# Layer 0 and feed-forward: short-row matmuls replaced by full 128-row f32r matmuls over stacked halves

## The chip, the cores and the metric

The kernel runs on one core of a Trainium2 chip. The metric is the time of one execution on the device, in microseconds. The engines that matter here, by the names of the profile: PE (TensorE, matmuls), ACT (ScalarE), DVE (VectorE), POOL (GpSimd) and SP, whose queue issues most of the transfers. Each engine works through its own queue in order.

## The reference

Four images of 128 channels and 64 x 64 pixels go through two layers. Cut to what matters (layer 1 is attention with a feed-forward, and then a recurrence along the tokens):

```python
# layer 0, on the group-normalised image
e1  = prelu(w1 @ x + b1, a1)          # 64 x 4096
e2  = prelu(w2 @ x + b2, a2)          # 64 x 4096
asm = prelu(wa @ x + ba, aa)          # 128 x 4096
score = softmax(einsum('nci,ncj->nij', e1, e2), axis=2)
x = x + einsum('nij,ncj->nci', score, asm)
# layer 1, on tokens (4096 per image): 16 heads of 8, then
x1 = ln(x + attn_out, g1, beta1)
zf = cos(x1[..., :8]) * cos(ry_theta)
h  = relu(zf @ w1.T + b1)             # 8 -> 512
out = ln(x1 + h @ w2.T + b2, g2, beta2)
```

The scores of layer 0 contract over 64 channels, and the first matmul of the feed-forward contracts over 8.

## The kernel before

The images are taken one after the other, and each has two stages.

**Layer 0** (`first_stage`, which calls `layer0`). The image lies as 128 channels x 4096 tokens. It is normalised (L340), and then two 1x1 convolutions give e1 and e2, in four pairs of 512-column blocks each (L352; the pairs' PSUM tiles are called pca and pcb). Each uses the 64 weights twice over, so that both halves of the 128 partitions hold the same 64 rows. `prelu` is two relus on ACT (L303, L304) and one combining step on DVE (L305). A third convolution gives asmT, with tokens on partitions: a bias matmul of one row (L360) and then the product (L369). `prelu_vector` (L309, L310) does every other one of its prelus on DVE alone.

Then come eight blocks `ic` of 512 tokens. For each, 16 steps `jp` compute the scores of 2 x 128 other tokens (L396, into a pair of PSUM banks called s), take their exponential on ACT (L404, tile p), add p up on DVE (L409, L412), and multiply p by asmT (`weigh`, L419, into acc). Two steps' scores stand together, followed by the two earlier steps' weighing. The scores are f32 matmuls of 64 rows; j = 0 uses partitions 0 to 63 and j = 1 uses 64 to 127.

Into this loop other work is woven by calls of `meanwhile`, which the code counts: the own block's normalisation and transposes (`tokens`), and, for images 1 to 3, the feed-forward of the image before (`feed_forward`, stepped by `step_late`, from the call after the twelfth on). The feed-forward's first matmul is L1049, its second L1060:

```python
            for j in range(2):
                rows = ds(32 * (f0 + j), D)
                nc.tensor.matmul(phs[j], f1_sb[rows, :], zT[rows, :], start=True, stop=True)
```

D is 8: eight rows of weights against 512 tokens, in eight chunks per image. Its ACT relu is L1052, the tile is hT.

**Attention** (`second_stage`, `attention`): scores of four heads in 32-row tiles of f32r (L879), exponentials on ACT (L891), transposes on DVE (L698), and two kinds of weighted sums on PE (L711, L732). At the end of the stage, POOL adds up the parts of each of three blocks of queries (`mirrored`: L774 copies, L759, L799 copies and L801 additions, in tiles called other, room and own). This runs on beside the start of the next image's layer 0, and the results are taken up there at three counted calls of `meanwhile`.

After the last image come its own feed-forward (`third_stage`), `fold_norm`, and the recurrence.

The engines' order in layer 0 is the order of the program (`tc.manual_schedule`). Every stage lays its tiles in SBUF anew, so a tile lies where earlier stages had others, and its first writer waits for the last user of those bytes. The first tiles of the layer-0 stage are the feed-forward's, then a tile called gap that nothing uses:

```python
        rest = dict(e=(BIG, 2), big=(BIG, 1), mid=(MID, 5))
        pools = {**ffn, "gap": ((P, GAP), 1), **rest, **sums}
```

Of the kernel before, what the change touches and what calls it, by code (L numbers as in the profile page):

```python
# [26 lines left out]
def kernel(  # L27
# [103 lines left out]
    GAP = 12 * IC  # L131
# [14 lines left out]
    def load_twice(ap, name, axis):  # L146

        shape = list(ap.shape)
        shape[axis] *= 2
        t = const.tile(shape, F32, tag=name, name=name)  # L150
        for i in range(2):
            part = t[:, ts(i, CR)] if axis else t[ts(i, CR), :]
            nc.gpsimd.dma_start(out=part, in_=ap)
        return t


    w1_sb, w2_sb = load_twice(w1T, "w1_sb", 1), load_twice(w2T, "w2_sb", 1)
    b1_sb, b2_sb = load_twice(b1, "b1_sb", 0), load_twice(b2, "b2_sb", 0)
    wa_sb = load(waT, "wa_sb")
    a1_sb, a2_sb, aa_sb = load_row(a1, "a1_sb"), load_row(a2, "a2_sb"), load_row(aa, "aa_sb")  # L160

    ba_row = const.tile([33, P], F32, tag="ba_row", name="ba_row")
    for i in range(2):
        nc.gpsimd.dma_start(out=ba_row[ds(32 * i, 1), :], in_=ba)
    for t in (a1_sb, a2_sb, aa_sb):
        nc.vector.tensor_scalar(t, t, -1.0, None, ALU.mult)
    minus_b = []
    for i, b in enumerate((b1_sb, b2_sb)):
        t = const.tile([P, 1], F32, tag=f"minus_b{i}", name=f"minus_b{i}")
        nc.vector.tensor_scalar(t, b, -1.0, None, ALU.mult)  # L170
        minus_b.append(t)
# [18 lines left out]
    f1_sb = const.tile([P, P], F32, tag="f1_sb", name="f1_sb")  # L190
    ry_sb = once.tile([P, 1], F32, tag="ry_sb", name="ry_sb")
    nc.gpsimd.memset(f1_sb, 0.0)
    nc.gpsimd.memset(ry_sb, 0.0)
    for f in range(NF):
        nc.scalar.dma_start(out=f1_sb[ds(32 * f, D), :], in_=f1T[:, ts(f, P)])
        nc.scalar.dma_start(out=ry_sb[ds(32 * f, D), :], in_=ry)
    fb1_sb, f2_sb, fb2_bc = load(fb1, "fb1_sb"), load(f2T, "f2_sb"), load_row(fb2, "fb2_bc")
    g1_bc, be1_bc = load_row(g1, "g1_bc"), load_row(be1, "be1_bc")
    g2_bc, be2_bc = load_row(g2, "g2_bc"), load_row(be2, "be2_bc")
    W_sb, WT_sb, VT_sb = load(W, "W_sb"), load(WT, "WT_sb"), load(VT, "VT_sb")  # L200
# [3 lines left out]
    nc.vector.tensor_tensor(fb2_bc, fb2_bc, be1_bc, ALU.add)  # L204
    ident = const.tile([P, P], F32, tag="ident", name="ident")
# [91 lines left out]
    nc.vector.tensor_scalar(f1_sb, f1_sb, cry, None, ALU.mult)  # L297
# [35 lines left out]
    def layer0(n, xs, xh, norm, shifted, begin, meanwhile):  # L333
# [11 lines left out]
        for e, w, b, a, name in (  # L345
            (e1, w1_sb, (b1_sb, minus_b[0]), a1_sb, "a"),
            (e2, w2_sb, (b2_sb, minus_b[1]), a2_sb, "b"),
        ):
            for i in range(NIC // 2):
                pc = pair_psum(f"pc{name}{n}_{i}")  # L350
                for j in range(2):
                    nc.tensor.matmul(pc[:, j, :], w, xh[:, ts(2 * i + j, IC)], start=True, stop=True)  # L352
                y, z = mid_tile(f"y{name}{n}_{i}"), mid_tile(f"z{name}{n}_{i}")
                prelu(e[:, ts(i, 2 * IC)].rearrange("p (a b) -> p a b", a=2), pc, y, z, b, a)
                meanwhile()
        asmT = big_tile(f"asmT{n}")
        for i in range(NIC // 2):
            pc = pair_psum(f"pa{n}_{i}")
            for j in range(2):
                nc.tensor.matmul(  # L360
                    pc[:, j, :],
                    ones[ds(32 * j, 1), :],
                    ba_row[ds(32 * j, 1), :].unsqueeze(1).broadcast_to([1, TG, P]),
                    start=True,
                    stop=False,
                    skip_group_check=True,
                )
            for k in range(2 * TG):
                nc.tensor.matmul(  # L369
                    pc[:, k // TG, ts(k % TG, P)],  # L370
                    xh[:, ts(2 * TG * i + k, P)],
                    wa_sb,
                    start=False,
                    stop=True,
                    skip_group_check=True,
                )
            to = asmT[:, ts(i, 2 * IC)].rearrange("p (a b) -> p a b", a=2)
            if i % 2:
                prelu_vector(to, pc, mid_tile(f"za{n}_{i}"), aa_sb)
            else:  # L380
                prelu(to, pc, mid_tile(f"ya{n}_{i}"), mid_tile(f"za{n}_{i}"), (0.0, 0.0), aa_sb)
            meanwhile()

        if shifted:

            nc.vector.memset(e2[CR : CR + 1, :], 1.0)
            for ic in range(NIC):
                row_max(n, ic, e1, e2)
        state = {}

        def scores(ic, jp):

            s = pair_psum(f"s{n}_{ic}_{jp}")
            for j in range(2):
                rows = slice(0, CR + 1) if shifted else ts(j, CR)
                nc.tensor.matmul(  # L396
                    s[:, j, :],
                    e2[rows, ts(2 * jp + j, P)],
                    e1[rows, ts(ic, IC)],
                    start=True,  # L400
                    stop=True,
                )
            p = mid_tile(f"p{n}_{ic}_{jp}")
            nc.scalar.activation(p, s, AF.Exp)  # L404
            if jp == 0:
                state["first"] = p
            elif jp == 1:
                total = get("sums", f"total{n}_{ic}")
                nc.vector.tensor_tensor(total, state["first"], p, ALU.add)  # L409
                state[ic] = total  # L410
            else:
                nc.vector.tensor_tensor(state[ic], state[ic], p, ALU.add)  # L412
            return p
# [20 lines left out]
        before = []  # L434
        for ic in range(NIC):
            for jp in range(0, NP, 2):
                fresh = [(ic, j, scores(ic, j)) for j in (jp, jp + 1)]
                for i in range(2):
                    if before:
                        weigh(*before[i])  # L440
                        if before[i][1] == NP - 1:
                            take(before[i][0])
                            begin(before[i][0], state)

                    meanwhile(2 if ic == NIC - 1 else 1)
                before = fresh
# [5 lines left out]
    def row_max(n, ic, e1, e2):  # L452

        maxima = once.tile([P, TG, 4], F32, tag="mx", name=f"mx{n}_{ic}")
        for it in range(TG):
            for jb in range(4):
                s = pair_psum(f"sm{n}_{ic}_{it}_{jb}")
                for j in range(2):
                    nc.tensor.matmul(
                        s[:, j, :],  # L460
                        e1[:CR, ts(TG * ic + it, P)],
                        e2[:CR, ts(2 * jb + j, IC)],
                        start=True,
                        stop=True,
                    )
                nc.vector.tensor_reduce(maxima[:, it, jb : jb + 1], s, AX.XY, ALU.max)
        nm = once.tile([P, TG], F32, tag="nm", name=f"nm{n}_{ic}")
        nc.vector.tensor_reduce(nm, maxima, AX.X, ALU.max, negate=True)
        pm = one_psum(f"pm{n}_{ic}")
        for k in range(TG):  # L470
            nc.tensor.matmul(
                pm[CR : CR + 1, ts(k, P)], nm[:, k : k + 1], ident, start=True, stop=True
            )
        nc.vector.tensor_copy(e1[CR : CR + 1, ts(ic, IC)], pm[CR : CR + 1, :])
# [509 lines left out]
    def feed_forward(im, i, t2_rows, last, final):  # L984
# [37 lines left out]
        be1_z = be1_bc[:, 0:D].unsqueeze(1).broadcast_to([P, TG, D])  # L1022
        nc.vector.tensor_tensor(z, blocks(v)[:, :, 0:D], be1_z, ALU.add)
        steps = cos_steps(zr, z, zk, zr)
        for _ in range(3):
# [6 lines left out]
        nc.vector.tensor_copy(  # L1032
            zs.rearrange("p (k r d) -> p k r d", k=TG, d=D),
            zr.unsqueeze(2).broadcast_to([P, TG, P // D, D]),
        )
# [4 lines left out]
        nc.scalar.copy(zT, pz)  # L1040
# [3 lines left out]
        for f0 in range(0, NF, 2):  # L1044
            phs = [one_psum(f"ph{n}_{i}_{f}") for f in range(f0, f0 + 2)]
            hs.append(get("hT", f"hT{n}_{i}_{f0}"))
            for j in range(2):
                rows = ds(32 * (f0 + j), D)
                nc.tensor.matmul(phs[j], f1_sb[rows, :], zT[rows, :], start=True, stop=True)  # L1049
# [57 lines left out]
    def fold_norm():  # L1107
# [88 lines left out]
    def first_stage(im, before):  # L1196
# [7 lines left out]
        rest = dict(e=(BIG, 2), big=(BIG, 1), mid=(MID, 5))  # L1204
# [3 lines left out]
        with stage(f"conv{n}", **pools, **psum), tc.manual_schedule(engines=engines):  # L1208
# [4 lines left out]
            def meanwhile(steps=1):  # L1213

                calls[0] += 1
                if before and calls[0] in (13, 16, 19):
                    before["left"].pop(0)()
# [3 lines left out]
                for _ in range(0 if calls[0] <= 12 else 2 if calls[0] % 8 == 0 else 1):  # L1221
                    step_late()
# [21 lines left out]
    def second_stage(im, tail, upcoming):  # L1244
# [5 lines left out]
            denom=((P, 2 * NT + NQB // 2 * TG, 2), 2),  # L1250
            later=((P, NT * 32), 2),
# [3 lines left out]
            fixed=((P,), 1),  # L1255
# [50 lines left out]
    def hold_every():  # L1306

        pool = ends.enter_context(tc.tile_pool(name="every", bufs=1))
        held["every"] = pool.tile([P, N, S], F32, tag="every", name="every")
        for n in range(N - 1):  # L1310
# [30 lines left out]
    with stage("fold", half=(HALF, 1), ps_one=(ONE, 1)):  # L1341
        fold_norm()
# [103 lines left out]
    with tc.If(any_bad > 0):  # L1446
# [5 lines left out]
        with stage(  # L1452
# [7 lines left out]
            fold_norm()  # L1460
# [90 lines left out]
```

## Time and profile before

| | |
|---|---|
| three runs | 7282.81, 7290.19 and 7290.84 us, median 7290.19 |
| span of the profiled execution, first to last instruction | 7288.0 us |
| PE busy | 7006.0 us, 96% of the span |
| DVE, ACT, POOL busy | 5902.5, 6018.3 and 2838.9 us |
| mean granted clock of PE | 0.982 |
| layer 0 of image 0 | about 20 to 430 us |
| attention of image 0 | about 430 to 1670 us |
| layer 0 of image 1, with the feed-forward of image 0 | about 1673 to 2200 us |
| last feed-forward, fold and recurrence | about 7030 to 7288 us |

The later images repeat the times of image 1 and of the first attention. A row of the costliest groups reads: line, engine, operation, output <- inputs, shapes, count | busy time, mean ns of one record | idle time of the engine just before, and what ended most of it. An f32 matmul leaves two records (two passes). Records of matmuls overlap, so their durations add up to more than the time they take; the distances between their starts don't. The timeline has start, duration, engine, line, operation, tiles, shapes and count.

### The profile page before, as it was taken

To read this page: it belongs to the slowest core of one execution; us is meant where nothing else is said; L and a number is where in the kernel's file an instruction comes from. 1 tells how busy PE (TensorE), PEld (TensorE's weight loads), DVE (VectorE), ACT (ScalarE), POOL (GpSimd) and SP (SyncE) were. 2 spreads that over 40 slices of the span, in tenths; PEclk is the share of its full clock that TensorE was granted. 3 is DMA by queue.
4 is the path that set the end of the run, shared out by engine and by line. 5 is a ranking of instruction groups with operands and counts; after the bars stand their busy time and mean duration, and the time that the engine had idled before them with its cause. 6 is when DMAs were issued, how large, how long until landed. Compare 5 with 4: busy or idle time off the path is not lost. (4 is left out here: it accounts for less than half of the span.)

```text
span 7288.0 us, 225126 instructions
## 1 busy us (share of the span) xinstructions
PE 7006.0 (96%) x93198; PEld 3501.8 (48%) x93198; DVE 5902.5 (81%) x7785; ACT 6018.3 (83%) x11936; POOL 2838.9 (39%) x10029
## 2 busy tenths in 40 slices
PE   8999999999999999999999999999999899999977
PEld 3445555554444555554444455555444355555546
DVE  5678899886668999888576999888866688899974
ACT  4479999995558999999555999999855599999976
POOL 0034444434223454444332354444432344444542
PEclk9999999999999999999999999999999999999988
DMA  0010000000111000000011100000001110000012
GB/s 28 32 35 24 30 20 21 21 16 20 39 41 36 27 21 20 21 23 20 21 35 44 37 21 20 21 26 20 17 25 38 40 36 21 21 26 27 11 59 105
DMA packets 83101, 212.81 MB, mean 29 GB/s; under 512 B 9120, under 2 KB 10432, under 8 KB 81296
## 3 DMA queue, kind: packets, MB, share of 16 engines
q1 hardware_dynamic: 77312, 186.68, 7.6%
q8 instruction: 733, 12.01, 0.7%
q10 hardware_dynamic: 4304, 11.43, 0.4%
q14 instruction: 304, 2.49, 0.1%
q0 software_dynamic: 448, 0.20, 0.0%
HBM read 141.65 MB, written 56.62 MB: 27 GB/s over the span
## 5 line engine op out<-in xcount | busy, mean ns | idle before, releaser
L891 ACT ACTIVATE e<-s 128x1024 f32<-128x1024 f32 (+1 forms) x3480 | 2949.1, 890 | 62.0 <-PE s L879 39.3
L698 DVE STREAM_TRANSPOSE t<-e 128x1024 f32<-128x1024 f32 x2240 | 2586.4, 1207 | 6.3 <-ACT e L891 3.9
L711 PEld LDWEIGHTS misc<-t,mirror 128*32 128x32 f32 x57344 | 1663.1, 110 | 1411.5 <-issue 1348.6
L711 PE MATMUL misc<-t,mirror 128*32 128x128 f32 x57344 | 1995.4, 273 | 28.6 <-DVE later L725 21.9
L891 ACT ACTIVATE xs<-s 128x1024 f32<-128x1024 f32 (+1 forms) x2152 | 1836.5, 894 | 32.2 <-PE s L879 19.5
L698 DVE STREAM_TRANSPOSE t<-xs 128x1024 f32<-128x1024 f32 x1344 | 1558.1, 1207 | 2.2 <-ACT xs L891 0.7
L732 PE MATMUL acc<-e,q_aug 128*32 128x512 f32 x11360 | 1518.6, 606 | 0.0
L879 PE MATMUL s<-queries,keys 32*128 32x512 f32 x9216 | 1216.9, 494 | 4.2 <-ACT e L891 2.9
L774 POOL COPY own<-o 32x36 f32<-32x36 f32 x2048 | 435.6, 213 | 1716.7 <-DVE o L766 1636.4
L419 PE MATMUL acc<-p,asmT 128*128 128x512 f32 x2048 | 976.3, 609 | 0.0
L732 PE MATMUL acc<-xs,q_aug 128*32 128x512 f32 x7072 | 942.2, 605 | 0.0
L412 DVE TENSOR_TENSOR total<-total,p 128x1024 f32<-128x1024 f32 x448 | 571.6, 1276 | 453.5 <-ACT p L404 430.4
L404 ACT ACTIVATE p<-s 128x1024 f32<-128x1024 f32 x512 | 497.3, 1021 | 512.0 <-PE s L396 511.0
L879 PEld LDWEIGHTS s<-queries,keys 32*128 32x128 f32 x9216 | 480.2, 182 | 490.4 <-issue 372.0
L668 POOL COPY mirror<-q 32x128 f32<-32x128 f32 x2048 | 608.7, 297 | 238.2 <-PE misc L711 150.5
L799 POOL COPY other<-turned 32x64 f32<-32x64 f32 x1904 | 449.5, 236 | 629.2 <-DVE turned L789 550.7
L891 ACT ACTIVATION_READ_ACCUMULATOR e<-s 128x1 f32 x2880 | 650.8, 226 | 0.0
L419 PEld LDWEIGHTS acc<-p,asmT 128*128 128x128 f32 x2048 | 362.2, 191 | 526.4 <-issue 518.0
L396 PE MATMUL s<-e,e 64*128 64x512 f32 x2048 | 538.2, 645 | 19.7 <-ACT p L404 12.5
L725 DVE TENSOR_TENSOR later<-later,misc 128x128 f32<-128x128 f32 (+1 forms) x576 | 162.4, 282 | 369.8 <-PE misc L711 365.9
L759 POOL COPY by_token<-by_key 32x4 f32<-32x4 f32 x2016 | 379.7, 188 | 85.1
L732 PEld LDWEIGHTS acc<-e,q_aug 128*32 128x32 f32 x11360 | 225.7, 108 | 347.4 <-issue 329.7
(244 smaller groups left out, 4801.6 us busy)
## 6 DMA issues: line engine op xcount, KB each, us to landing
keys<-parts_dram SPq DMA_DIRECT2D x256, 256.0 KB
queries<-parts_dram SPq DMA_DIRECT2D x1024, 32.0 KB
fx<-x_dram SPq DMA_DIRECT2D x64, 256.0 KB
x_dram<-x SPq DMA_DIRECT2D x56, 256.0 KB
xs<-in_x_dram SPq DMA_DIRECT2D x16, 512.0 KB
t_dram<-t2T SPq DMA_DIRECT2D x32, 256.0 KB
t2s<-t_dram SPq DMA_DIRECT2D x16, 512.0 KB
parts_dram<-high SPq DMA_DIRECT2D x28, 256.0 KB
```

The source lines that it names most:

```text
L396: nc.tensor.matmul(s[:, j, :], e2[rows, ts(2 * jp + j, P)], e1[rows, ts(ic, IC)], start=True, stop=True,)
L404: nc.scalar.activation(p, s, AF.Exp)
L412: nc.vector.tensor_tensor(state[ic], state[ic], p, ALU.add)
L419: nc.tensor.matmul(state["acc", ic], asmT[:, ts(2 * jp + j, P)], p[:, j, :], start=jp == 0 and j == 0, stop=jp == NP - 1 and j == 1,)
L668: nc.gpsimd.tensor_copy(wv[ts(a, 32), s, :, :, ts(a, D)], own[ts(s, 32)])
L698: nc.vector.transpose(group["e"][h][:, k, :], es[h])
L711: nc.tensor.matmul(state["acc"][ts(2 * x + h, 32), :], state["w"][:, QT * (s // 4) + TG * x + s % 4, h, :], state["e"][h][:, :, ds(IC * x ...
L732: nc.tensor.matmul(it["in"]["acc"][ts(2 * h + x, 32), :], it["qa"][:, ds((2 * it["tiles"][x] + h) * V, 32)], it["e"][h][:, ts(x, IC)], sta ...
L774: nc.gpsimd.tensor_copy(own[ts(s, 32), ts(x, 4), h, :], ov[ts(2 * h + x, 32), s, :, 0:V])
L799: copy(to[ts(k, 32), h], tv[ts(2 * x + h, 32), k])
L879: nc.tensor.matmul(ss[h][:, x, :], keys[unit[x] // QT].bitcast(F32R)[r, ts(unit[x] % QT, P)], queries[b].bitcast(F32R)[r, :], start=True, ...
L891: nc.scalar.activation(es[h][:, ts(x, IC)] if split else es[h], ss[h][:, x, :] if split else ss[h].rearrange("p x c -> p (x c)"), AF.Exp, ...
```

## The change

In layer 0:

- w1 and w2 stand side by side as one 128-column weight. One convolution gives both, e1's 64 rows above e2's (`both_convs`); its prelu has per-row slopes. From the result, ACT writes a copy rounded to f32r (the upper bits of the number), DVE subtracts it from the original to get what rounding left, and two DMAs per quarter on SP arrange the halves: the tile e2 becomes 64 rows of low half over 64 rows of high half, and the tile e1 holds e1 twice.
- `halves(ic)` splits each 512-token block of e1 in the same way, into a new pair of buffers hl.
- A score is then two f32r matmuls of 128 rows (e2's low and high half, against the high and then the low half of e1) in place of one f32 matmul of 64 rows. The two row-tiles of before are gone.
- The bias of the third convolution becomes a 128-row f32r matmul, with the two halves of the bias in rows 0 and 32. Both convolutions alternate in one loop, with eight counted calls of `meanwhile` in place of twelve.
- gap shrinks from 12 to 7.5 times 512 floats, to make room for hl.

In the feed-forward, z is split into two halves on DVE, and the weights f1 are multiplied out, split and stacked at the start of the program, so that L1049 is one f32r matmul of 128 rows. W is loaded later. In the attention stage, the pool `fixed` stands ahead of `later`.

```diff
-    GAP = 12 * IC
+    GAP = 15 * IC // 2
...
+    nc.vector.tensor_scalar(f1_all, f1_all, cry, None, ALU.mult)
+    f1_high = f1_sb.rearrange("p f e -> p (f e)")
+    nc.vector.tensor_copy(f1_high.bitcast(F32R), f1_all)
+    nc.vector.tensor_tensor(f1_low, f1_all, f1_high, ALU.subtract)
+
+    nc.sync.dma_start(out=f1_high[ds(2 * D, 2 * D), :], in_=f1_low[ds(2 * D, 2 * D), :])
...
+        def both_convs(i):
+
+            cols = ts(i, 2 * IC)
+            pc = pair_psum(f"pc{n}_{i}")
+            for j in range(2):
+                nc.tensor.matmul(
+                    pc[:, j, :], w12_sb, xh[:, ts(2 * i + j, IC)], start=True, stop=True
+                )
+            y, z = mid_tile(f"y{n}_{i}"), mid_tile(f"z{n}_{i}")
+            prelu(pair(e1[:, cols]), pc, y, z, (b12_sb, minus_b12), a12_sb)
+            nc.scalar.copy(pair(e2[:, cols]).bitcast(F32R), pair(e1[:, cols]))
+            low = y[CR:P]
+            nc.vector.tensor_tensor(low, pair(e1[CR:P, cols]), pair(e2[CR:P, cols]), ALU.subtract)
+            nc.sync.dma_start(out=pair(e2[0:CR, cols]), in_=low)
+            nc.sync.dma_start(out=e1[CR:P, cols], in_=e1[0:CR, cols])
...
-                    ones[ds(32 * j, 1), :],
-                    ba_row[ds(32 * j, 1), :].unsqueeze(1).broadcast_to([1, TG, P]),
+                    ones.bitcast(F32R),
+                    ba_rows.bitcast(F32R).unsqueeze(1).broadcast_to([P, TG, P]),
...
+        for i in range(NIC // 2):
+            both_convs(i)
             meanwhile()
...
+            third_conv(i)
+            meanwhile()
...
+        def halves(ic):
+
+            hl = get("hl", f"hl{n}_{ic}")
+            src = e1[:, ts(ic, IC)]
+            nc.vector.tensor_copy(hl[:, 0, :].bitcast(F32R), src)
+            nc.vector.tensor_tensor(hl[:, 1, :].bitcast(F32R), src, hl[:, 0, :], ALU.subtract)
...
         def scores(ic, jp):
...
             for j in range(2):
-                rows = slice(0, CR + 1) if shifted else ts(j, CR)
-                nc.tensor.matmul(
-                    s[:, j, :],
-                    e2[rows, ts(2 * jp + j, P)],
-                    e1[rows, ts(ic, IC)],
-                    start=True,
-                    stop=True,
-                )
+                parts = [(e2.bitcast(F32R)[:, ts(2 * jp + j, P)], hl[:, y, :]) for y in range(2)]
...
+                for y, (stationary, moving) in enumerate(parts):
+                    nc.tensor.matmul(
+                        s[:, j, :], stationary, moving, start=y == 0, stop=y == len(parts) - 1
+                    )
...
-        nc.vector.tensor_copy(
-            zs.rearrange("p (k r d) -> p k r d", k=TG, d=D),
-            zr.unsqueeze(2).broadcast_to([P, TG, P // D, D]),
-        )
+        nc.vector.tensor_copy(z.bitcast(F32R), zr)
+        nc.vector.tensor_tensor(zr, zr, z, ALU.subtract)
+        zv = zs.rearrange("p (k r y d) -> p k r y d", k=TG, y=2, d=D)
+        for y, part in enumerate((z, zr)):
+            nc.vector.tensor_copy(
+                zv[:, :, :, y, :], part.unsqueeze(2).broadcast_to([P, TG, P // (2 * D), D])
+            )
...
-                rows = ds(32 * (f0 + j), D)
-                nc.tensor.matmul(phs[j], f1_sb[rows, :], zT[rows, :], start=True, stop=True)
+                nc.tensor.matmul(
+                    phs[j],
+                    f1_sb[:, f0 + j, :].bitcast(F32R),
+                    zT.bitcast(F32R),
+                    start=True,
+                    stop=True,
+                )
...
-        rest = dict(e=(BIG, 2), big=(BIG, 1), mid=(MID, 5))
+        rest = dict(e=(BIG, 2), hl=(MID, 2), big=(BIG, 1), mid=(MID, 5))
...
-                if before and calls[0] in (13, 16, 19):
+                if before and calls[0] in (9, 12, 15):
...
-                for _ in range(0 if calls[0] <= 12 else 2 if calls[0] % 8 == 0 else 1):
+                for _ in range(0 if calls[0] <= 8 else 2 if calls[0] % 8 == 0 else 1):
...
+            fixed=((P,), 1),
             later=((P, NT * 32), 2),
```

## The prediction

> **What bounds the kernel now.** I read the shares of busy time first, then the costliest groups, then the timeline of the stages that the change touches.
>
> ```profile
> span 7288.0 us, 225126 instructions
> PE 7006.0 (96%) x93198; PEld 3501.8 (48%) x93198; DVE 5902.5 (81%) x7785; ACT 6018.3 (83%) x11936; POOL 2838.9 (39%) x10029
> ...
> L879 PE MATMUL s<-queries,keys 32*128 32x512 f32 x9216 | 1216.9, 494 | 4.2 <-ACT e L891 2.9
> ...
> L419 PE MATMUL acc<-p,asmT 128*128 128x512 f32 x2048 | 976.3, 609 | 0.0
> ...
> L396 PE MATMUL s<-e,e 64*128 64x512 f32 x2048 | 538.2, 645 | 19.7 <-ACT p L404 12.5
> ```
>
> TensorE sets the time: 282 us of idle in 7288. By windows it is busy 360.7 of 365 us in the layer-0 loop of image 0 (55 to 420), 452.0 of 490 in that of image 1 (1690 to 2180), where the previous image's feed-forward runs inside it, and 1149.1 of 1150 in an attention stage (470 to 1620). In image 1's loop its largest waits are on other engines ("pt <- DVE t" 12.5 us, "pc <- ACT hT" 5.4), so I count PE time saved there at 0.85 and in image 0 at all of it. A record's mean (645 ns) isn't a price, since records overlap; starts are. One steady group of image 0, on PE:
>
> ```profile
> 154.79 0.65 PE L496 MATMUL sum<-total,ones 128*32 128x128 f32 x16
> 155.36 1.99 PE L396 MATMUL s<-e,e 64*128 64x512 f32 x8
> 157.28 1.98 PE L419 MATMUL acc<-p,asmT 128*128 128x512 f32 x4
> 159.10 0.60 PE L282 MATMUL pt<-ident,taken 128*128 128x128 f32 x4
> ```
>
> The eight score records take 157.28 - 155.36 = 1.92 us. The single starts lie 429 ns apart, each a pair of 64-row tiles that run together: 4 x 429 = 1.72. The other 0.20 is the change from 64-row tiles to full ones; the change back costs the same before the group. The half-used array is thus already used by pairs, and the change can't halve this time: that is what one has to see before the rest.
>
> **The Trainium skill.** "TensorE: Matmul & The Clock Gate", section "Wait — 56ns, not 53.3ns?": warm matmuls start N/2.4 GHz + 2.5 ns apart, 215.7 ns at 512 columns. The trace agrees as far as it goes: a group of four 32-row f32r matmuls (L879) takes 431 ns with two changes of mode in it, so 216 to 234 ns without. It shows no f32r matmul of 128 rows. "TensorEngine Tiling (Array Packing)", section "Key Properties": a change of tiling mode drains TensorE; the trace gives 0.197 us each. "SBUF — State Buffer", section "SBUF: two separate sides": VectorE in a two-port mode and GpSimd lock one another out. It agrees: the same eight copies of L799 take 2.14 or 4.06 us, below.
>
> **A. Scores of layer 0.** Per two steps of jp: out go 1.718 us of f32 pairs and two mode changes, 0.394; in come eight full f32r passes (four blocks of j, high and low half of e1). The pass has no row. Below: 213 ns, the 512 columns at one per cycle, what the L879 group supports. Above: 298 ns; at half clock, at 436.65, an L879 record lasts 788 ns against 490, so no more than 298 can scale with the clock. I take 216 (the page's price, and the low end of the L879 reading): 8 x 216 = 1.728. So 0.010 - 0.394 = -0.384 us per group. There are 64 groups per image; in 8 the 32-column sum L496 stands beside the scores and one change stays: 56 x 0.384 + 8 x 0.187 = 23.0, I say 22. Images: 22 + 3 x 22 x 0.85 = **-78 us**. At 298 ns a group would cost +0.27 us: +60 to +70. The two answers meet at 264 ns.
>
> **B. First feed-forward matmul** (L1049). A group of four 8-row f32 passes takes 1.057 us, two per chunk; after, 2 x 216 = 0.432. Saved 2 x 0.625 = 1.25 us, in 24 chunks that run inside layer 0: 24 x 1.25 x 0.85 = **-25**. In the last feed-forward (8 chunks, 7030 to 7145) PE is busy only 74 of 115 us and waits for "pw <- ACT cT" 18.9: of 10 us I count **-6**. L1060, the second matmul, stays.
>
> **C. Convolutions.** Two 64-output convs become one: 8 x 2 passes of 429 ns, 6.9 us per image, and the bias matmul L360 falls from 1.06 to 0.43 per pair. But this stretch is a round trip PE - ACT - DVE: ACT does two relus (1.11 us each), DVE the combining step L305 (1.28). Before, 33.4 us pass from the first L305 (1682.55) to the first weighing (1715.96). After: half as many relus for e1 and e2, but a copy to f32r on ACT (1.02), a subtraction on DVE (half the rows, about 1.2), two 256 KB DMAs on SP per quarter, and the halves (1.25 us) before the first score. By these rows 33 us. So 0, bounds -8 and +8 (per image -2 to +2): a late DMA of e2 or e1 would hold the first score.
>
> **D. What the first e1 write waits for.** Here is what I think decides the sum. The layer-0 stage has a dummy tile "gap" at its front, which holds e1 and e2 off the bytes that the end of attention still reads. The new hl buffers (8 KB a partition) shrink it from 12 to 7.5 x 512 floats. By the addresses in the built kernels e1 began behind `room` and `other`; now it lies over them. By the waits in the built kernel the first write of e1 (DVE) in images 1 and 3 waits for the second L801 of room0, and in image 2 for the last L801 of room1, on POOL. This is POOL before, in image 1:
>
> ```profile
> 1678.87 3.52 POOL L759 COPY by_token<-by_key 32x4 f32<-32x4 f32 x16
> 1682.43 4.06 POOL L799 COPY other<-turned 32x64 f32<-32x64 f32 x8
> 1686.57 0.44 POOL L801 TENSOR_TENSOR own<-own,other 128x128 f32<-128x128 f32 x1
> ...
> 1692.94 6.43 POOL L759 COPY by_token<-by_key 32x4 f32<-32x4 f32 x16
> 1699.41 3.04 POOL L799 COPY room<-room 32x64 f32<-32x64 f32 x8
> 1702.54 0.44 POOL L801 TENSOR_TENSOR own<-own,room 128x128 f32<-128x128 f32 x1
> 1703.04 2.14 POOL L799 COPY room<-room 32x64 f32<-32x64 f32 x8
> 1705.26 0.44 POOL L801 TENSOR_TENSOR own<-own,room 128x128 f32<-128x128 f32 x1
> ```
>
> and this DVE:
>
> ```profile
> 1682.55 1.28 DVE L305 SCALAR_TENSOR_TENSOR e<-za,a_sb,ya 128x1024 f32<-128x1024 f32 x1 [1.44 <-ACT za L304]
> ```
>
> DVE would stand from 1682.5. Behind it wait its own queue, ACT (the copy into e2 is next there) and PE (both pc buffers full). With DVE silent POOL runs at its quiet prices: `other` 2 x (2.14 + 0.44) + 0.2, by_token 0.2 + 3.52, room0 2 x 2.58, so from 1682.43 to about 1697: **14.5 us**. Image 2 does room1 too, 0.2 + 3.5 + 5.2 more: about 24. POOL at its pace of before would give 23, 34 and 24 (first L305 at 1682.55, 3467.22, 5253.35; the L801 ends at 1705.7, 3501, 5277). Nothing can hide it: PE has no other work here, since the feed-forward starts only after the convs. I take 14.5 + 24 + 14.5 = **+53**; bounds 0 and +81. TensorE's clock may drop after a stall that long: +3, bounds 0 and 10.
>
> **E. Other edits.** The halves add two DVE operations (about 1.25 us, 32 times), split and rounding of z 0.5 us 32 times, all beside PE work on a DVE that is busy 323 of 490 us; where DVE already ends a wait ("pt <- DVE t") they lengthen it: +3, bounds 0 and 15. At the start f1's product, rounding, subtraction and an SP DMA stand ahead of the normalisation L340 on DVE: it starts at about 25 instead of 20.9, and image 0's convs give part of it back: +2, bounds -3 and +6. Loading W late, on POOL's queue, is hidden by the whole last stage. The layout of attention ("fixed" moved) changes no matmul there: 0.
>
> **Sum.** -78 - 25 - 6 + 0 + 53 + 3 + 3 + 2 = -48. The profiled span is 7288.0, 2 us below the median of 7290.2 and inside the three runs (7282.8 to 7290.8). 7288 - 48 = 7240: I say **7240 us**. 0.2%, 15 us, is about what a measurement of this kernel can tell from no change.
>
> **Rivals.**
> 1. *The gain without the stall.* If POOL is done when DVE comes to the first e1 write, or the waits sit later than I read, -48 - 56 = -104: **7185**. For it: POOL's copies are fast when DVE is quiet. Against: 14 us of them still stand ahead.
> 2. *The waits eat it.* The layer-0 loops with feed-forward become bound by DVE and ACT (323 and 257 of 490 busy, in order on each queue), so images 1 to 3 give 0.4 rather than 0.85, and the stall is the longer one: -22 - 27 - 12 - 3 + 81 + 8 = +25 at worst, with either alone **7265 to 7280**. Against: PE's waits there sum to 38 us only.
> 3. *Slower: a full 128-row f32r pass costs more than a 32-row one.* From 264 ns the scores lose, and from about 245 (each ns is 8 x 256 = 2 us over the scores, so -48 is gone after 24 to 29 ns) the change does. At 298: 82 x 2 x 0.9 = +148, less 48: **7390**. For it: no row shows the pass, and L879 writes from four row tiles at once, so its price is an inference. Against: 431 ns leaves only 234 even for the L879 group with the smallest mode cost.
> 4. *Nothing in the scores*: mode changes that the trace puts at 0.197 us hidden otherwise. The regular 1.92 against 1.72 speaks against it; about 7315.
>
> **How the numbers follow.** My case 0.50 (7215 to 7265), rival 1 0.17 (7170 to 7215), rival 2 0.17 (7265 to 7310), rivals 3 and 4 0.16 (7300 to 7400). From 7180 to 7305 some 0.8 is held. Faster by over 0.2% (below 7275.6): all of my case and of rival 1, a third of rival 2: 0.72. Within 0.2%: 0.11. Slower: 0.17.
>
> **What would show it.** Group of scores: eight starts 216 ns apart, the group about 1.73 us and no gap before the weighing; 250 or more is rival 3. The first e1 write of images 1 to 3: DVE idle 14, 24 and 14 us, released by POOL L862; no idle is rival 1. The ph group: 0.43 us a pair. PE's idle in images 1 to 3 grown by more than the stalls: rival 2. The attention stages should last what they did; if they don't, the reckoning by stages is wrong.

## The result, and the profile after

The changed kernel takes 7289.5 us (median of 12 runs) against 7288.1 before (12 runs): a ratio of 1.0003, interval 0.9995 to 1.0012. It is the same to within a tenth of a per cent, where 48 us less were forecast. The profiled execution has a span of 7287.8 us, against 7288.0.

The page of the kernel after, its first lines and the rows that answer to those shown of before:

```profile
span 7287.8 us, 224891 instructions
...
PE 6887.5 (95%) x92974; PEld 3739.8 (51%) x92974; DVE 5937.1 (81%) x7949; ACT 6003.1 (82%) x11919; POOL 2845.1 (39%) x10025
...
L463 PE MATMUL acc<-p,asmT 128*128 128x512 f32 x2048 | 955.5, 599 | 0.0
...
L444 PE MATMUL s<-hl,e 128*128 128x512 f32 x2048 | 615.5, 445 | 40.8 <-DVE hl L427 25.0
```

TensorE is busy 118.5 us less (7006.0 - 6887.5), and the span is the same: all of it went into idle time. The row of the scores says one place: PE stands 25 us for `hl`. To find the others I read the starts of each stage off the timeline, in both kernels. "Head" is the time from the normalisation's start to the first weighing of an image (in images 1 to 3 it is counted from the last step of the normalisation factors, 0.8 us earlier, in every kernel alike), "loop" from there to the end of the last weighing. All stage times below are of the profiled executions, one of each kernel.

| stage | before, us | after, us | difference | forecast |
|---|---|---|---|---|
| start of the first normalisation | 20.9 | 23.9 | +3.0 | +2 |
| heads of images 0 to 3 | 39.2, 44.2, 47.4, 44.0 | 39.9, 61.0, 70.3, 61.9 | +58.3 | +56 (D with its clock) |
| loops of images 0 to 3 | 367.0, 494.0, 495.4, 496.9 | 354.2, 475.9, 476.5, 478.2 | -68.5 | -100 (A, B, E) |
| attention, four stages | 4974.9 | 4977.0 | +2.1 | 0 |
| last feed-forward up to the recurrence | 157.0 | 162.7 | +5.7 | -6 |
| sum | | | +0.6 | -48 |

The recurrence, which the table leaves out, is 0.8 us shorter; so the spans differ by -0.2.

The stall was there, at the place and nearly at the price that the forecast gave it. Image 1's DVE in the kernel after, by the timeline (start, duration, engine, line, and in brackets the idle time before and its releaser):

```profile
1672.85 0.73 DVE L850 STREAM_TRANSPOSE room<-later 128x256 f32<-128x256 f32 x2
1688.81 1.28 DVE L327 SCALAR_TENSOR_TENSOR e<-z,a_sb,y 128x1024 f32<-128x1024 f32 x1 [15.22 <-POOL own L862]
```

and POOL in the same stretch:

```profile
1679.84 3.52 POOL L820 COPY by_token<-by_key 32x4 f32<-32x4 f32 x16
1683.40 2.13 POOL L860 COPY room<-room 32x64 f32<-32x64 f32 x8
1685.61 0.44 POOL L862 TENSOR_TENSOR own<-own,room 128x128 f32<-128x128 f32 x1
1686.11 2.15 POOL L860 COPY room<-room 32x64 f32<-32x64 f32 x8
1688.34 0.44 POOL L862 TENSOR_TENSOR own<-own,room 128x128 f32<-128x128 f32 x1
```

The second L862 of room0 ends at 1688.78 and e1's first write starts at 1688.81. With DVE still, POOL runs at its quiet prices throughout (2.13 us for eight copies, 3.52 for by_token). The same wait in images 2 and 3, from the table of DVE's waits (total, times, longest):

```profile
DVE e L327 <- POOL own L862: 25.3, 1, 25.3
```

```profile
DVE e L327 <- POOL own L862: 15.8, 1, 15.8
```

15.2 + 25.3 + 15.8 = 56.3 us. And a fourth place, which the forecast didn't have. The SP queue loads fx for the last feed-forward; before and after:

```profile
7028.94 3.65 SPq L997 DMA_DIRECT2D fx<-x_dram  x8
```

```profile
7038.11 11.79 SPq L1058 DMA_DIRECT2D fx<-x_dram  x8
```

The attention ends 5.1 us earlier in the kernel after, and yet the loads start 9 us later. 7038.11 is when POOL has done with room0 there too (its second L862 runs from 7037.65 to 7038.09).

What was gained per group of scores is seen where nothing else stands between, late in image 1's loop. Before and after, on PE:

```profile
2119.69 1.99 PE L396 MATMUL s<-e,e 64*128 64x512 f32 x8
2121.61 3.70 PE L419 MATMUL acc<-p,asmT 128*128 128x512 f32 x8
2125.24 1.99 PE L396 MATMUL s<-e,e 64*128 64x512 f32 x8
```

```profile
2120.25 2.41 PE L444 MATMUL s<-hl,e 128*128 128x512 f32 x8
2122.49 3.60 PE L463 MATMUL acc<-p,asmT 128*128 128x512 f32 x8
2125.53 2.40 PE L444 MATMUL s<-hl,e 128*128 128x512 f32 x8
```

A round, from one group of scores to the next, was 5.55 us and became 5.28; the median of the undisturbed rounds is 5.26. Eight weighing records take 8 x 0.429 = 3.43 us of it, and 1.83 are left for the eight score passes: 228.5 ns each. The profile puts the start of the first f32r record some 0.4 us too early (here 3.04 us after the first of eight weighing records), so only whole rounds are compared.

### The profile page after: what moved, and what is told of

The parts are those of the page before. It is cut to its first block, busy times and chain, and to the rows that moved or that the text cites. A ratio compares the mean times of both kernels' runs of the same rounds, so it can differ in the third digit from the quotient of the medians.

```text
span 7287.8 us, 224891 instructions
## 1 busy us (share of the span) xinstructions
PE 6887.5 (95%) x92974; PEld 3739.8 (51%) x92974; DVE 5937.1 (81%) x7949; ACT 6003.1 (82%) x11919; POOL 2845.1 (39%) x10025
## 5 line engine op out<-in xcount | busy, mean ns | idle before, releaser
L463 PE MATMUL acc<-p,asmT 128*128 128x512 f32 x2048 | 955.5, 599 | 0.0
L444 PE MATMUL s<-hl,e 128*128 128x512 f32 x2048 | 615.5, 445 | 40.8 <-DVE hl L427 25.0
L463 PEld LDWEIGHTS acc<-p,asmT 128*128 128x128 f32 x2048 | 385.1, 192 | 338.9 <-issue 316.5
L444 PEld LDWEIGHTS s<-hl,e 128*128 128x128 f32 x2048 | 400.0, 199 | 201.8 <-issue 99.4
L786 DVE TENSOR_TENSOR later<-later,misc 128x128 f32<-128x128 f32 (+1 forms) x576 | 162.7, 282 | 373.6 <-PE misc L772 370.7
```

The lines of the kernel that those rows point to most:

```text
L444: nc.tensor.matmul(s[:, j, :], stationary, moving, start=y == 0, stop=y == len(parts) - 1)
L463: nc.tensor.matmul(state["acc", ic], asmT[:, ts(2 * jp + j, P)], p[:, j, :], start=jp == 0 and j == 0, stop=jp == NP - 1 and j == 1,)
```

## The experiments

Every ratio is to the kernel before on the same chip, whose medians were 7283.8 to 7286.6.

**1. Put `fixed` back** (on the changed kernel).

```diff
-            fixed=((P,), 1),
             later=((P, NT * 32), 2),
...
             other=((P, QT * 2 * D), 1),
+            fixed=((P,), 1),
```

> The changed kernel with one edit: the pool `fixed` stands behind `other` again, so later, room and other lie below the bytes of e1. Theory (the order of the pools makes the stall): the DVE idle of about 17, 23 and 18 us before the first weighing of images 1 to 3 goes, and so does the 9 us by which the last stage's fx loads start late. 7289.5 - 58 - 6 = about 7225. Rival (the shrunk gap is the cause, as the prediction had it): the first write of e1 still waits for POOL, nothing moves, 7289. Second rival (the loops behind gave back what they gain, whatever stands before them): the stall goes but PE's waits grow, 7260 or more.

7221.2 us, ratio 0.9913 (0.9896 to 0.9929). The heads are 40.2, 44.1, 45.1 and 47.2 us, as before the change, and the last feed-forward takes 150.5 instead of 162.7: 57 + 12 us. Its fx loads start 5.1 us after the last weighted sum of attention, as in the kernel before (19.3 us in the changed kernel):

```profile
6965.90 3.65 SPq L1058 DMA_DIRECT2D fx<-x_dram  x8
```

So one line about an order of pools, which changes no instruction's work, cost 68 us. The loops are the same as in the changed kernel (352.9, 478.0, 476.6, 475.9): what they miss has another cause.

**2. The short gap alone** (on the kernel before).

```diff
-    GAP = 12 * IC
+    GAP = 15 * IC // 2
```

> The kernel before with one edit: gap is 7.5 instead of 12 times 512 floats. Theory (order of the pools and gap act only together): e1 comes down onto the old places of the mirror tiles, which are done with, so no wait: 7288, within 0.1%. Rival (the prediction's reading: the gap alone uncovers the stall): three waits of 14 to 24 us, about 7341.

7288.1, ratio 1.0001 (0.9992 to 1.0009). Nothing. The forecast took the gap for the cause, and alone it is none.

**3. The order of the pools alone** (on the kernel before): the same move of `fixed` as in the change, gap left at 12.

> The kernel before with one edit: `fixed` stands ahead of `later`, gap stays at 12. Theory (only together): by the addresses only image 2's first write of e1 waits, for the second addition of room0 on POOL (about 14 us), and the last stage's fx loads start 9 us late (some 6 us): about 7308. Rival (the order of the pools alone is the cause): all three stalls, 7350. Rival (no effect without the short gap): 7288.

7308.8, ratio 1.0031 (1.0020 to 1.0042), as expected. The head of image 2 is 61.8 us (47.4), the others are unmoved, and the last feed-forward takes 167.5 (157.0). In image 2, the table of DVE's waits has the one line:

```profile
DVE e L305 <- POOL own L801: 14.9, 1, 14.9
```

`fixed` holds two tiles each of q_aug and mirror, 21 KB a partition. With it ahead, the tiles behind it (`later` with room1, `half` with room0, turned and other) stand 21 KB higher, by the addresses at the bytes where the next stage puts e1 and where the last one puts fx. The order makes the overlap; the short gap lets e1 reach more of it, so that three images wait where one did.

**4. Price the scores** (on experiment 1): f32, 64 rows, two row tiles, no halves.

```diff
-                parts = [(e2.bitcast(F32R)[:, ts(2 * jp + j, P)], hl[:, y, :]) for y in range(2)]
+                rows = ts(j, CR)
+                parts = [(e2[rows, ts(2 * jp + j, P)], e1[rows, ts(ic, IC)])]
```

> e1_fixed_back with the scores of layer 0 as f32 matmuls of 64 rows in two row tiles again, and without the halves of e1; the arrangement of e1 and e2 stays, so the scores leave out the low half for one of the two row tiles (the output is not the reference's). It prices the score part alone, against e1_fixed_back. By the distances of starts a group takes 5.55 us in this form and 5.26 in f32r. If the gain comes through: 56 x 0.29 = 16 us in image 0 and about 14 in each of images 1 to 3, so e1_fixed_back + 58. If PE's waits on DVE and ACT eat it in images 1 to 3: e1_fixed_back + 15 to 30. If a full f32r pass had cost 216 ns: + 80.

7254.2, ratio 0.9958 (0.9941 to 0.9974): the f32r scores with their halves are worth 33 us, not 78. By stages, f32r makes the four loops 14.2, 10.4, 11.7 and 15.5 us shorter (51.8), and the four heads 5.3, 4.8, 4.2 and 9.0 us longer (23.3); the profiled execution (7249.0) was 5 us quicker than the median.

**5. Take that wait out of the head** (on experiment 1): `halves(0)` ahead of the last quarter's convolutions.

```diff
         for i in range(NIC // 2):
+            if i == NIC // 2 - 1 and not shifted:
+                halves(0)
             both_convs(i)
...
-        if not shifted:
-            halves(0)
```

> e1_fixed_back with one edit: the halves of the first block of e1 are made ahead of the last quarter's convolutions, not after the last asmT. In e1_fixed_back PE waits 6 us for `hl` before the first score, and starts cold. Theory (that wait is what the f32r scores cost ahead of the loop): the phase from the normalisation to the first weighing falls from 40 to 47 us to near the 35 to 41 us of e4_f32_scores, in each image: about 7203. Rival (the second score pair waits for the PSUM pair of the last asmT anyway): 1 to 2 us per image, 7215.

7220.2, ratio 0.9908 (0.9892 to 0.9925): no gain over experiment 1, although the heads did fall to 34.6, 38.3, 39.0 and 39.6. The loops of images 1 to 3 took it back: 483.1, 486.1, 482.9. Neither theory had that. DVE's waits at the start of image 1's loop, in experiment 1 and in this one:

```profile
DVE v L1069 <- POOL own L862: 3.4, 1, 3.4
```

```profile
DVE v L1069 <- POOL own L862: 8.6, 1, 8.6
```

v is the first product of the feed-forward; its tile lies over room1, and POOL is not done with that before 1709 (here 1704). A head that ends earlier runs into POOL's end. The wait reaches PE through ACT, which normalises v and stands for it, with the next exponential (p) behind it in its queue:

```profile
1712.41 1.65 ACT L284 ACTIVATE v<-v,less_v,r_v 128x128 f32<-128x128 f32 x4 [9.13 <-POOL less_v L277]
```

```profile
1715.02 3.78 PE L446 MATMUL s<-hl,e 128*128 128x512 f32 x8 [4.11 <-ACT p L450]
```

PE stands 4.1 us (1.4 at the like place in experiment 1), and the eight passes behind it take 3.78 us where others take 2.4: they start 427 ns apart. By the time of the 33rd weighing record the loops of images 1 to 3 are 5.3 to 5.8 us behind experiment 1, most of what they lose in all.

**6. Price the feed-forward's first matmul** (on experiment 1).

```diff
-                    f1_sb[:, f0 + j, :].bitcast(F32R),
-                    zT.bitcast(F32R),
+                rows = ds(32 * (f0 + j), D)
+                nc.tensor.matmul(phs[j], f1_sb[rows, f0 + j, :], zT[rows, :], start=True, stop=True)
```

> e1_fixed_back with the feed-forward's first matmul as f32 of 8 rows again (it reads rows 32 f to 32 f + 7 of the new stacked weights, most of them zero, so the feed-forward is not computed). It prices that part alone. By starts it costs 1.25 us with both mode changes against 0.47 for two f32r passes: 1.57 us per chunk. If all came through: 24 x 1.57 = 38 in the loops and some 6 in the last stage, 7265. If PE's waits take half of it: 7245. If the chain of the feed-forward sets the pace whatever PE takes: 7225.

7275.3, ratio 0.9985 (0.9978 to 0.9991): 54 us more than experiment 1, and more than the highest of the expectations. The loops of images 1 to 3 are 15.5, 13.7 and 18.9 us longer (48), the last feed-forward 8.9. PE is busy 46 us longer in these loops; the price by starts accounts for 38 of it, and the other 8 were not taken apart.

**7. The same score matmuls in bf16** (on experiment 1).

```diff
+                e2b = e2.bitcast(BF16).rearrange("p (s t) -> p s t", t=2)
+                parts = [(e2b[:, ts(2 * jp + j, P), 1], hlb[:, y, :, 1]) for y in range(2)]
```

> e1_fixed_back with the same score matmuls reading the upper 16 bits of each number as bf16, both operands with a step of 4 bytes (so the scores keep 8 bits of each half; what is left out is the rest of the mantissa). It asks why a full f32r pass takes 229 to 235 ns and not 216. If f32r itself costs the 18 ns: passes of 216 ns, 8 x 0.018 us x 256 = 37 us less on PE, 7190. If it is the weight load or the stream of load and matmul: passes stay at 234, 7221.

7218.4, ratio 0.9908 (0.9892 to 0.9925). Eight passes take 1.80 us, 225 ns each (starts in a stretch of image 0: 225, 224, 225, 226, 225, 224 apart), against 228.5 in f32r. So the number type makes a difference of some 4 of the 12 ns above 216; the rest is there in bf16 with this step of 4 bytes too. What it is (the load of 128 columns before every pass and the step are candidates) was not taken apart.

**8. Move a step of distance** (on experiment 1). The feed-forward is written as a generator: at each `yield` the loop goes on with its own work, so a `yield` is one step of distance between the instruction that makes a tile and the PE transposes that read it. One `yield` less between zs (the copies of z) and its transposes, one more ahead of the transposes of t (the chunk's result).

> e1_fixed_back with one step of the feed-forward's distance moved: one less between zs and its transposes, one more ahead of the transposes of t. PE waits 16 us per image for t there. Theory (the waits grew because the distances are counted in groups, and a group is 0.29 us shorter): the wait on t falls by 5 to 10 us per image, 7195 to 7206, less what pz then waits. Rival (a wait only moves to the next link of the chain): 7221, within 5.

7281.6, ratio 0.9993 (0.9986 to 1.0000): 60 us worse. PE's waits in image 1's loop, in experiment 1 and in this one:

```profile
PE pt L292 <- DVE t L1150: 16.2, 5, 5.7
```

```profile
PE pz L292 <- DVE zs L1097: 29.2, 4, 10.1
...
PE pt L292 <- DVE t L1149: 2.6, 2, 1.8
```

The wait for t fell by 14 us, more than the theory asked for; the one for zs rose to 29, from under 1.

**9. Early halves and a later feed-forward** (on experiment 5).

```diff
-                if before and calls[0] in (9, 12, 15):
+                if before and calls[0] in (12, 15, 18):
...
-                for _ in range(0 if calls[0] <= 8 else 2 if calls[0] % 8 == 0 else 1):
+                for _ in range(0 if calls[0] <= 11 else 2 if calls[0] % 8 == 0 else 1):
```

> e5b_early_halves with the feed-forward's first step three calls of `meanwhile` later (after 11 instead of 8; the results of `mirrored` taken up at calls 12, 15 and 18). In e5b the phase ahead of the loop became 5.6 to 7.6 us shorter, and the loops of images 1 to 3 became 5 to 10 us longer: DVE waits 8.6 us for POOL's last addition of room1 (3.4 in e1_fixed_back) at the feed-forward's first v. Theory (POOL's end is the second cover of that start): with the first v later the wait goes and the loops return to 473 to 477 us, 7190 to 7200. Rival (what e5b gave back is TensorE's half clock at the start of the loop): 7220.

7189.6, ratio 0.9869 (0.9852 to 0.9885), the quickest of all. DVE's wait for POOL at v is gone from its table, the heads stay short (34.3, 40.5, 39.5, 42.9) and the loops are 473.0, 473.3 and 473.2. POOL's end was what took back experiment 5's gain: by the 33rd weighing record the loops have regained 5.0, 3.4 and 3.1 us. The other 21 us that they gain on experiment 5 come later in the loop, where the later start has shortened other waits (in image 1, t from 16.0 to 10.3 us, `last` ahead of pwx from 5.5 to 2.9). The later start without the early halves was not run, so how much of the 31 us it would give alone stays open.

**10 and 11. One more step ahead of t**, alone on experiment 1, and on experiment 9.

> e1_fixed_back with one more step of distance ahead of the transposes of t, and none taken away elsewhere. In e8b the wait for t fell from 16 to 2.6 us per image, and the wait for zs rose to 29. Theory (distance is what both lack, and the loop has steps to spare, since the feed-forward ends 70 us before it): the wait for t falls by 13 us in each of three images, loops of 462 to 468 us, 7180 to 7195. Rival (the longer chain of a chunk holds back the next, two at most being under way): 7221 or more.

7210.8, ratio 0.9899 (0.9882 to 0.9915): 10 us of the expected 26 to 41. The wait for t fell from 16.2 to 5.1 us, and that for zs rose to 11.8 without anything taken from its own distance. That two chunks are under way in step, and a longer chunk moves them against each other, is a reading that no run tests.

> Early halves, the later start of the feed-forward and the added step together. If they add up: 7221 - 25 - 35 = about 7160. If one covers the other: the better of e9_early_late and e10_yield_added.

7193.0, ratio 0.9874 (0.9857 to 0.9890): they don't add up. It is no better than experiment 9 without the added step.

**12. Without the split of z** (on experiment 1): the copy into zs of the kernel before.

> e1_fixed_back without the split of z: one copy on DVE fills zs as in the kernel before, so the low half of z is left out and the high half is counted twice. From e4_f32_scores and e6b_ph_8row, the score part is worth 38 us and the feed-forward's matmul 48 us in the loops of images 1 to 3, but both together only 56: some 10 us per image are lost to something that both those kernels share with e1 and not with the kernel before. Theory (it is the split of z, three more DVE operations between the cosine and the transposes that PE waits for): loops of 466 to 468 us, 7191. Rival (the operations are hidden, the loss is in the clock or in other waits): within 5 us of e1_fixed_back, 7221.

7222.2, ratio 0.9913 (0.9897 to 0.9930), against 7221.2 with the split: it costs nothing that can be seen.

**13 and 14. The place of the double steps**, on experiment 1 and on experiment 9. At every eighth call of `meanwhile` the feed-forward is stepped twice.

```diff
-                for _ in range(0 if calls[0] <= 8 else 2 if calls[0] % 8 == 0 else 1):
+                for _ in range(0 if calls[0] <= 8 else 2 if calls[0] % 8 == 4 else 1):
```

> e1_fixed_back with the feed-forward's double steps at calls of `meanwhile` whose number leaves 4 when divided by 8, not 0. The convolutions now count eight calls and not twelve, so this puts the double steps back at the 4th and 12th call of each block of the loop, as in the kernel before. Theory (the shift by four calls costs the missing 10 us per image): loops of 466 to 470 us, about 7193. Rival (the place does not matter): within 5 us of 7221.

7215.4, ratio 0.9904 (0.9887 to 0.9920): the loops of images 1 to 3 fall by 7 us together, a quarter of what is missing. One wait goes entirely, PE's for `last` ahead of pwx. In image 1's loop, in experiment 1 and in this one (the kernel before has 0.7 too):

```profile
PE pwx L1170 <- ACT last L1229: 6.3, 4, 2.2
```

```profile
PE pwx L1170 <- ACT last L1229: 0.7, 1, 0.7
```

Others grow in its place: that for q (L612) from 2.4 to 4.6 us, that for z (L1084) from 0.8 to 3.0.

> e9_early_late (7189.6) with the double steps moved by four calls in the same way; its feed-forward starts three calls later, so the places are not those of the kernel before. If the distance to the block's own work matters as such, its loops of 473 us change by several us in one direction or the other: 7165 to 7215. If not, within 5 us of 7190.

7197.4, ratio 0.9879 (0.9862 to 0.9895): 8 us the other way. The place matters by a few us, in either direction.

## Why the prediction was wrong, point by point

**Where the sum went wrong.** Forecast were -48 us, measured +1.4. By the table, 31.5 us are missing in the loops (A, B and E), 11.7 in the last feed-forward, and some 5 in the other rows. Two steps failed. One is in the sum of A and B: PE time saved in the loops was put at 118 us (22 + 3 x 22 for the scores, 30 for the feed-forward), and 103 of it, 87%, was to come through. In experiment 1, PE is busy 91.6 us less in the loops, and 69.9, 76%, came through; in images 1 to 3 it is 73% in place of 85%. The other is E's zero for the move of `fixed`, which cost the last feed-forward 12.2 us (and which, with the short gap, made the stall of D, where it was counted as the work of the gap).

**What bounds the kernel** was read rightly: the score group fell by its mode changes alone, and the attention stages lasted what they did, within 2 us of 4975.

**A, the scores, failed in the price of one term.** I had two values for a full f32r pass: the Trainium skill's 215.7 ns ("TensorE: Matmul & The Clock Gate", "Wait — 56ns, not 53.3ns?") and 216 to 234 from the L879 group, and took the page's. The measured price is 228.5 ns, 1.828 us for eight, and the measurement decides. The low end of the L879 reading was a misreading: 431 ns lie between the first start of that group and of the next, so one change of mode stands in it and not two. If that change costs what it does at the scores, 431 - 197 = 234 are left, and nothing in the trace gave 216. 8 x 12.5 ns x 256 groups = 26 us on PE. The mode changes (0.39 us a group) came as priced: 5.55 - 0.29 = 5.26.

**A also had a cost that stood in C at 1.25 us per image.** The halves of the first block don't merely take 1.25 us: in DVE's queue they stand behind the last quarter's asmT, so PE waits 6.3 us for them (the 25 us of the L444 row, four times), and its next sixteen passes start 427 ns apart, not 228.5 (image 0, 56.5 to 63.8 us). Experiment 4 puts it at 23 us in the four heads, and experiment 5, which moves the halves alone, takes 25 us out of them. Merging the convolutions gained 21 there (heads of 34.9, 39.3, 40.9 and 38.2 in experiment 4 against the kernel before), so C's sum of 0 held by luck, from two terms of 20 that cancel.

**B, the feed-forward, was too small**: -31 forecast, 54 measured when it alone is undone. Of the mode changes, 1.057 us holds only the one that leaves; the one that enters lies in the record before. With it a chunk saves 1.57 us and not 1.25, and undone alone all of PE's time came through. In the loops the two parts, each undone alone, are worth 51.8 us (A, 78 forecast) and 48 (B, 25): their sum of 100 meets the forecast 103 by luck, since one was too large and the other too small. What is missing is that both together give only 70.

**D was right in place and price, and wrong in its cause.** 53 forecast, 56.3 measured, with POOL at its quiet prices and the waits on the instructions that the built kernel named. But the text put it on the smaller gap, and under E it priced the move of `fixed` at 0 because no matmul of attention changes. A pool's place is no matter of its own stage: it decides what the next stage's tiles lie on. Experiments 2 and 3 show that the gap alone costs nothing, the order alone 21 us, and both 68.

**The last stage, forecast at -6, came at +5.7.** It is the same step: the move of `fixed` was put at nothing without a look at the tiles that it displaces there. Experiment 1 gives back 12.2 us, and with that the stage is 6.5 us shorter than before, as B had it. What loading W later costs was not tested.

**The rivals.** The waits that eat the gain (rival 2) were the nearest in time, but at 73% of PE's time in images 1 to 3 and not the 40% that it named. The gain without the stall (rival 1, -104) was not there to be had either: with the stalls gone, experiment 1 gains 65 us. The price of the pass (rival 3) was the right term to doubt; at 228.5 it took a third of A and didn't turn the sign of it. The range's upper end, 7305, held the result; the likeliest case did not.

**What stays open.** In the loops of images 1 to 3 the score part gives 38 us and the feed-forward part 48, each undone alone, but both together 56 against the kernel before: 10 us per image are lost to something that experiments 1, 4, 6 and 12 share. Of these 30 us, 18 are PE's waits and 12 longer busy time on PE. It is not the split of z (12). A wait that all four have and the kernel before has not is PE's for `last` ahead of pwx, 5.5 to 7.1 us per loop against 0.7. Experiment 13 shows what sets it, the place of the double steps; but since other waits grow when it goes, that is worth only 2 of the 10. What the other 8 are was not isolated.

## What to carry to other kernels

Where stages reuse memory, an edit of a pool's order or size is an edit of the next stage's waits: compare the addresses of the tiles first written there with those of the tiles last read before, and ask it of each stage, not only of the one where a stall is seen. When a price is read from a trace, ask which changes of mode stand in it before taking a table's as confirmed. Two savings priced one by one need not add up: here 100 us were 70 together. And a saved microsecond counts only up to the next limit: here the earlier end of the head was worth nothing until the step that waited for POOL was put later too.

## What the runs showed of the hardware

A 128-row pass of 512 columns in a stream where each pass loads its own 128 columns of weights started 228.5 ns after the one before in f32r and 225 ns in bf16 (read with a step of 4 bytes). An f32 pass of the same shape, of which a matmul has two, takes 429 in the same loop. After PE had stood for 6.3 us, sixteen such f32r passes started 427 ns apart. So splitting an f32 matmul of 64 rows, two in row tiles, into two f32r matmuls of 128 rows left PE's time almost as it was (1.72 and 1.83 us per eight); what paid was that the tiling mode no longer changed, at 0.2 us a change (5.55 - 3.43 - 1.72 = 0.40 us for the two of a round).
